# A graph-attention layer: spreading the maxima in four wide products, and issuing the gathers in one piece at the head of a step

## The chip, the cores and the metric

The kernel runs on one core of one Trainium2 chip. The metric is the device time of one execution in microseconds (us); lower is better. The time before is the median of three runs, 1335.21 us, with the runs between 1331.93 and 1343.83 us. Five engines work beside each other, each through its own instruction queue in program order: TensorE (PE), VectorE (DVE), ScalarE (ACT), GpSimd (POOL) and SyncE (SP). Transfers are issued from SP, ACT and POOL.

## The reference

Inputs are 3125 nodes with 128 features, 100000 edges (`src`, `dst`, sorted by `dst`) and for each edge one of five types. For each type `r` the reference computes an 8-head attention over the edges of that type, and adds the five results:

```
q, k, v = x[dst] @ W_Q[r], x[src] @ W_K[r], x[src] @ W_V[r]        # per edge, 8 heads of 16
logits  = (q * k).sum(-1) / 4 + attn_bias[r]
max_v   = segment_max(logits of type r, dst)
exp_l   = exp(logits - max_v[dst])                                  # 0 for other types
attn    = exp_l / (segment_sum(exp_l, dst)[dst] + 1e-12)
out    += segment_sum(attn * v, dst)
```

After that come an output projection with bias, a residual, a layer norm with gain and shift, a second residual with `x` and a second layer norm.

## The kernel before, in words

**Prologue.** All keys and values for each (node, type) pair are computed first and stored in DRAM as `kv_d`: row `5 * node + type`, 256 numbers (K, then V). The queries go to `q_d` in three bf16 parts that add up to the exact number. The list of rows to gather for each edge lies in SBUF as `idx[p, t, g]`.

**Groups and windows.** The edges, sorted by destination, are cut into 196 groups of 512 (`NGR`, `GE`): four columns `t` of 128 edges (`T = 4`). The destinations of one group lie within 25 nodes, so a group touches at most 125 rows (25 nodes by 5 types) of `q_d` and of the table of maxima `m_d`.

**The loop.** Loop step `k` works on several groups at different stages; which groups is fixed by `group_at`, `v_at`, `full_step`, `ready` and `done_at`, and the order of calls in the body of `for k in range(...)` is the program order on every engine. For a group `g` the stages are:

- `gather` (POOL, L681): four indirect DMAs bring the K and V rows of 4 x 128 edges into the ring of buffers `kvs_[g % KVB]`. The first `KVA` groups are gathered ahead of the loop; in the loop, step `k` issues those of group `k + AHEAD`, `AHEAD` being 2. The first two of a group are issued after `weigh`, the other two after `logits`, and these two take their row numbers from a small copy `rows` that VectorE makes (L692).
- `spot` (DVE, L746) makes `hot`, a 0/1 matrix that says which of the 125 rows each edge belongs to; `spread_q` (PE, L755) multiplies `hot` by the three parts of the queries, so that each edge has its query, `qe`.
- `logits` (DVE, L768 and L769), in step `g`: product of keys and queries, then a sum over each head; `store_logits` (SP) writes them to `lg_d`.

When all logits of a block of 128 nodes are there, in step `full_step[b]`, the block's maxima follow. `maxima_load` (POOL, L781) fetches the logits by node into `ell` with one indirect DMA, in step `full_step[b] + 1`. `maxima` (DVE and ACT, L796 to L840) takes the masked maxima in three pieces at the end of steps `full_step[b] + 2` to `+ 4`; its first instructions, `by_head` on ACT and `mine` on DVE, wait for `ell`. The result, in three bf16 parts for each head, is stored to `m_d` (`store_m`) and read back by group (`fetch_m`, tile `mw`).

Then the same edges come by a second time, as group `v`. From group 22 on, that is 19 steps after their logits:

- `spread_m` (PE, L872), one step ahead: `hot` times the three parts of the maxima, accumulated in PSUM, gives each edge its maximum, tile `me`. The operand repeats the 8 heads `times` times (8 times in the loop, so 64 columns; 12 times after the last group), and only the first repetition is read.
- `less_max` (DVE, L881) and `exps` (ACT, L885): the exponentials, written in place over `me` in PSUM.
- `weigh` (DVE, L890), in step `at_k[v]`: values times exponentials, to `wv`. It is the last reader of the group's gathered buffer. `weights` (ACT, L898) copies the exponentials beside them.
- `places` (ACT), `sums` (PE, L924 and on), `norm` (DVE, L945 to L948), `carry` and `by_node`: sums by row, division, sum over the types.

**What ties the gathers to the rest.** With `KVB = 21` buffers, the gathers of group `k + 2` go into the buffer of group `k - 19`, which `weigh` releases in step `k` itself. The copies `rows` and the gathers that read them are also tied: the second half of the gathers of group `k + 2` can't start before DVE has passed `logits` of step `k`. On POOL's queue the order is: the first two gathers of group `k + 2`, the other two, then, once every eight steps, `maxima_load`.

Of the kernel before, what the change touches and what calls it, by code (L numbers as in the profile page):

```python
# [17 lines left out]
P = 128  # L18
# [4 lines left out]
HEADS = 8  # L23
# [17 lines left out]
T = GE // P  # L41
NGR = -(-E // GE)
# [4 lines left out]
WR = WN * R  # L47
# [6 lines left out]
AHEAD = 2  # L54
# [5 lines left out]
SB = P * E // N // SR  # L60
SPAD = 5
QB = 3
KVB = 21
HELD = 21
KVA = 6


@with_exitstack
# [61 lines left out]
NM = len(MB)  # L130


def windowed_path(
# [4 lines left out]
    nc = tc.nc  # L138
# [4 lines left out]
    kv_d = dram.tile([((NT - 1) * P + 64) * R, KVW], F32, name="kv_d")  # L143
# [208 lines left out]
    live = {}  # L352
# [290 lines left out]
    rows, counted = {}, 0  # L643
# [29 lines left out]
    ps = ctx.enter_context(tc.tile_pool(name="ps", bufs=2, space=PSUM))  # L673
    buffers(i for i in range(KVB) if i not in at_once)
    hold = ctx.enter_context(tc.tile_pool(name="hold", bufs=HELD))
    flow = ctx.enter_context(tc.tile_pool(name="flow", bufs=2))
    late_flow = ctx.enter_context(tc.tile_pool(name="late_flow", bufs=2))
    def gather(g, t0, rows):
        kv = kvs_[g % KVB]
        for t in range(T // 2):  # L680
            nc.gpsimd.indirect_dma_start(  # L681
                out=kv[:, t0 + t, :], out_offset=None, in_=kv_d[:, :],
                in_offset=bass.IndirectOffsetOnAxis(ap=rows(t), axis=0),
            )

    def first_gathers(g):
        gather(g, 0, lambda t: idx[:, t, g : g + 1])

    def more_gathers(g):

        rows = flow.tile([P, T // 2], I32, name="rows", bufs=3)
        nc.vector.tensor_copy(rows, idx[:, T // 2 :, g])  # L692
        gather(g, T // 2, lambda t: rows[:, t : t + 1])


    def fetch_x(name, b):
# [68 lines left out]
    def logits(g):  # L765
        kv, lg = kvs_[g % KVB], live["lg", g]
        prod = flow.tile([P, T, H], F32, name="prod", bufs=1)
        nc.vector.tensor_tensor(prod, kv[:, :, :H], live.pop(("qe", g)), op=ALU.mult)  # L768
        nc.vector.tensor_reduce(  # L769
            lg[:, :, :HEADS], prod.rearrange("p t (k d) -> p t k d", d=HD), AX.X, ALU.add  # L770
        )
# [7 lines left out]
    def maxima_load(b):  # L779
        ell = late_flow.tile([P, D, LW], F32, name="ell", bufs=1)  # L780
        nc.gpsimd.indirect_dma_start(  # L781
            out=ell.rearrange("p s c -> p (s c)"), out_offset=None,
            in_=lg_d[: (full_at(MEND[b], D) + 1) * GE, :],
            in_offset=bass.IndirectOffsetOnAxis(ap=start_i[:, b : b + 1], axis=0),
        )
        live["ell", b] = ell
# [78 lines left out]

    def spread_m(g, times):

        me = ps.tile([P, T, times, 2, HEADS // 2], F32, name="me", tag="me")
        hot, mw = live.pop(("hot", g)), live.pop(("mw", g))
        for t in range(T):  # L870
            for s in range(3):
                nc.tensor.matmul(  # L872
                    me[:, t], hot[:, t, :],
                    mw[:WR, None, :, s, :].to_broadcast([WR, times, 2, HEADS // 2]),
                    start=(s == 0), stop=(s == 2),
                )
        live["mde", g] = me[:, :, 0].rearrange("p t h k -> p t (h k)")

    def less_max(g):
        mde = live["mde", g]  # L880
        nc.vector.tensor_tensor(mde, live.pop(("lg", g))[:, :, :HEADS], mde, op=ALU.subtract)  # L881

# [4 lines left out]
    def weigh(g):  # L887
        wv, kv = late_flow.tile([P, T, PW], F32, name="wv"), kvs_[g % KVB]
        live["wv", g] = wv
# [66 lines left out]
    def by_node(g):  # L956
        f = window(g, first, ACTE)
        nc.scalar.copy(oT[:, bass.ds(f, WN)], live.pop(("op", g)))
# [68 lines left out]
    step_of, n = {}, 0  # L1027
# [3 lines left out]
    group_at = {k: g for g, k in step_of.items()}  # L1031
    final = step_of[NGR - 1]
# [5 lines left out]
    full_step = [step_of[full_at(n, D)] for n in MEND]  # L1038
# [3 lines left out]
    at_k, k = {}, 0  # L1042
    for v in range(NGR):
        k = max(k + 1, ready[block_of(v, MEND)])
        at_k[v] = k
    v_at = {k: v for v, k in at_k.items()}
# [19 lines left out]

    gathered = 0
    for gathered in range(KVA):
        first_gathers(gathered)
        gather(gathered, T // 2, lambda t: idx[:, T // 2 + t, gathered : gathered + 1])  # L1070
    assert all(q_from[b] >= 2 for b in range(QB, NT))
    for k in range(-2, root_at[NT] + 2):
        v, g = v_at.get(k), group_at.get(k)
        q_step = {k - f: b for b, f in enumerate(q_from) if b >= QB and -2 <= k - f <= 5}

        if k >= 0 and k + 3 in group_at:
            fetch_keys(group_at[k + 3])
            fetch_q(group_at[k + 3])
        if -2 in q_step:
            fetch_x("xq", q_step[-2])  # L1080
        for b in range(NT):
            if done_at[b] - 1 == k:
                fetch_x("xr", b)
            if norm_at[b + 1] + 1 == k:
                store_z(b)
        for b in range(NM):
            if ready[b] - 3 == k:
                store_m(b)
        if 5 in q_step:
            store_q(q_step[5])  # L1090
        for u in range(NGR):
            if max(at_k[u] - 3, ready[block_of(u, MEND)] - 2) == k:
                fetch_m(u)

        for b in range(NT):
            if done_at[b] + 1 == k:
                residual(b)
        if v_at.get(k - 4) is not None:
            by_node(v_at[k - 4])
        if v_at.get(k - 2) is not None:  # L1100
            carry(v_at[k - 2])
        if 1 in q_step:
            turned(q_step[1])
        if 3 in q_step or 4 in q_step:
            second_part()
        if 2 in q_step or 3 in q_step:
            first_part()

        if v_at.get(k + 1) is not None:
            spread_m(v_at[k + 1], 8 if k + 1 in group_at else 12)  # L1110
        if v_at.get(k - 1) is not None or v_at.get(k - 3) is not None:
            sums(v_at.get(k - 1), v_at.get(k - 3))
        if k + 1 in group_at:
            spread_q(group_at[k + 1])

        if v is not None:
            weigh(v)
        ahead_of = []
        while gathered < NGR - 1 and step_of[gathered + 1] <= k + AHEAD:
            gathered += 1  # L1120
            ahead_of.append(gathered)
            first_gathers(gathered)
        if v_at.get(k + 1) is not None:
            less_max(v_at[k + 1])
            exps(v_at[k + 1])
        if v is not None:
            weights(v)
        if k + 1 in group_at:
            types(group_at[k + 1])
        if v_at.get(k - 2) is not None:  # L1130
            norm(v_at[k - 2])
        if g is not None:
            logits(g)
            store_logits(g)
        for u in ahead_of:
            more_gathers(u)
        for b in range(NM):
            if full_step[b] + 1 == k:
                maxima_load(b)
        if k + 2 in group_at:  # L1140
            spot(group_at[k + 2])
        if v_at.get(k + 1) is not None:
            places(v_at[k + 1], 2 if k >= final - 1 else 0)
        if 3 in q_step or 4 in q_step:
            third_part()
        if 2 in q_step or 3 in q_step:
# [528 lines left out]
```

## Time and profile before

| | us |
|---|---|
| median of three runs | 1335.21 |
| lowest and highest run | 1331.93, 1343.83 |
| the profiled execution: its own time | 1331.93 |
| the profiled execution: its span, first to last instruction | 1330.1 |
| busy: PE, DVE, ACT, POOL | 873.1, 958.6, 633.8, 802.4 |
| mean granted TensorE clock | 0.762 |

The span is one execution on the core. "Busy" is the time with an instruction of that engine running. An idle time is put down to the thing that ended it, written `A <- B`. A line such as L681 is a line of the kernel above. The chain that ended last is followed back from the last instruction, at each step to what released it.

The execution has four stretches: the prologue to 84 us, a start-up in which gathers are issued back to back to about 240 us, the steady loop until the last gather is issued at 1243.84 us, and an end without gathers.

### The profile page before, as it was taken

Reading aid. Unit: us, or ns where it says so; the run is one execution under the profiler, and the core shown is the slowest. Engines: PE = TensorE matmul, PEld = TensorE weight load, DVE = VectorE, ACT = ScalarE, POOL = GpSimd, SP = SyncE. Lnnn points to the kernel's source line nnn. Section 1 sums busy time; section 2 is a strip of 40 time slices with the busy share of each in tenths; the row PEclk is TensorE's granted clock in tenths of the full one; section 3 lists DMA queues with packets and bytes.
Section 4 is the critical chain, followed back from the end, with each engine's and each line's share of the span. In section 5 each row is a group of like instructions: output and inputs, shape, how many; then the busy total and the mean of one; then the engine's idle time right before and its main releaser. Section 6 shows DMA issues by size and latency. Waiting matters only on the chain.

```text
span 1330.1 us, 26045 instructions
## 1 busy us (share of the span) xinstructions
PE 873.1 (66%) x7526; PEld 685.6 (52%) x7526; DVE 958.6 (72%) x2749; ACT 633.8 (48%) x2248; POOL 802.4 (60%) x901
## 2 busy tenths in 40 slices
PE   7974356576667676665757656667766677676595
PEld 3543244455455555544645545555545565565474
DVE  4554557768777876876976876877787687687786
ACT  2650034355446445445545545545644544544354
POOL 2637776666667667567656656766766766666300
PEclk9985577787688778778777868877767866776787
DMA  6986676566566556456556556656645655655300
GB/s 171 352 301 169 160 180 147 151 167 157 137 158 167 133 152 170 124 153 175 128 146 168 149 132 162 153 145 163 165 135 150 177 131 146 168 138 136 82 10 17
DMA packets 180892, 203.66 MB, mean 153 GB/s; under 512 B 83207, under 2 KB 146083, under 8 KB 180620
## 3 DMA queue, kind: packets, MB, share of 16 engines
q0 software_dynamic: 40896, 113.39, 29.6%
q1 hardware_dynamic: 135414, 83.80, 26.2%
q10 hardware_dynamic: 4430, 4.71, 1.4%
q8 instruction: 63, 1.03, 0.3%
q14 instruction: 89, 0.73, 0.2%
HBM read 166.50 MB, written 35.28 MB: 152 GB/s over the span
## 4 chain that ended last, share of the span: by engine, by line
DVE 34%; PE 21%; DMA 20%; issue 12%; POOL 7%; ACT 4%; SPq 2%; DVEq 0%; ACTq 0%; POOLq 0%
DMA ell<-lg_d,start_i 8%; POOL kv L681 7%; PE pp L924 6%; DVE wl L819 5%; DVE prod L768 4%; DMA mw<-m_d 4%; DVE wv L890 4%; PE pr L395 3%; DVE mx L825 3%; PE me L872 3%; DVE lg L769 3%; DVE hot L746 2%; PE qe L755 2%; ACT by_head L796 2%; DMA kv<-kv_d,rows 2%
## 5 line engine op out<-in xcount | busy, mean ns | idle before, releaser
L681 POOL DMA_INDIRECT kv<-kv_d,idx x404 | 383.8, 950 | 261.8 <-DVE den L945 142.8
L681 POOL DMA_INDIRECT kv<-kv_d,rows x380 | 363.8, 957 | 131.9 <-issue 76.6
L924 PE MATMUL pp<-wv,at 128*125 128x136 f32 x1568 | 357.6, 362 | 1.0 <-DVE o L948 1.0
L924 PEld LDWEIGHTS pp<-wv,at 128*125 128x125 f32 x1568 | 267.8, 236 | 66.1 <-issue 64.2
L910 ACT ACTIVATE at<-row_at,nkey 128x125 f32<-128x125 f32 x744 | 237.5, 397 | 0.0
L755 PE MATMUL qe<-qw,hot 125*128 125x128 bf16 x2352 | 206.9, 251 | 40.9 <-DVE hot L746 36.5
L872 PE MATMUL me<-mw,hot 125*128 125x64 bf16 (+1 forms) x2352 | 125.7, 210 | 143.6 <-DMA mw<-m_d 69.5
L755 PEld LDWEIGHTS <-hot 125*128 125x128 bf16 x2352 | 194.0, 123 | 47.4 <-DVE hot L746 44.1
L885 ACT ACTIVATE me<-me 128x32 f32<-128x32 f32 x196 | 35.7, 182 | 365.8 <-DVE me L881 364.7
L872 PEld LDWEIGHTS <-hot 125*128 125x128 bf16 x2352 | 112.9, 109 | 176.4 <-DVE wv L890 77.1
L926 PE MATMUL pp<-pt,carried 125*5 125x136 f32 x390 | 96.0, 337 | 135.4 <-ACT pt L939 135.0
L768 DVE TENSOR_TENSOR prod<-kv,qe 128x512 f32<-128x512 f32 x196 | 133.1, 679 | 61.5 <-DMA kv<-kv_d,rows 49.5
L769 DVE TENSOR_REDUCE lg<-prod 128x32 f32<-128x512 f32 x196 | 134.4, 686 | 6.8
L890 DVE TENSOR_TENSOR wv<-kv,me 128x512 f32<-128x512 f32 x196 | 132.2, 675 | 4.9 <-PE pp L924 4.3
L913 ACT ACTIVATE at<-at 128x500 f32<-128x500 f32 (+1 forms) x196 | 117.3, 598 | 6.2
L716 PE MATMUL prq<-wq,xTq 128*128 128x384 f32 (+1 forms) x88 | 51.4, 680 | 98.5 <-DVE rem L726 98.5
L926 PEld LDWEIGHTS pp<-pt,carried 125*5 125x5 f32 x390 | 18.2, 86 | 174.2 <-ACT pt L939 153.4
L796 ACT COPY by_head<-ell 128x512 f32<-128x512 f32 x24 | 25.7, 1071 | 139.9 <-DMA ell<-lg_d,start_i 139.9
L804 DVE SCALAR_TENSOR_TENSOR mine<-slot,deg,ell 128x64 f32<-128x64 f32 x25 | 8.4, 336 | 115.5 <-DMA ell<-lg_d,start_i 115.5
L881 DVE TENSOR_TENSOR me<-lg,me 128x32 f32<-128x32 f32 x196 | 37.3, 191 | 74.4 <-PE me L872 70.7
L819 DVE TENSOR_TENSOR wl<-by_head,shut 128x1024 f32<-128x1024 f32 (+2 forms) x73 | 76.9, 1053 | 11.5 <-ACT by_head L796 9.3
L746 DVE TENSOR_SCALAR hot<-kt,row_of 125x512 bf16<-125x512 bf16 x196 | 82.7, 422 | 1.5 <-DMA kv<-kv_d,idx 1.0
(186 smaller groups left out, 1210.7 us busy)
## 6 DMA issues: line engine op xcount, KB each, us to landing
kt<-key_d SPq DMA_DIRECT2D x196, 128.0 KB
qw<-q_d SPq DMA_DIRECT2D x196, 96.0 KB
kv_d<-kvs SPq DMA_DIRECT2D x24, 640.0 KB
q_d<-q SPq DMA_DIRECT2D x22, 480.0 KB
kv<-kv_d,idx POOLq DMA_INDIRECT x404
kv<-kv_d,rows POOLq DMA_INDIRECT x380
lg_d<-lg SPq DMA_DIRECT2D x196, 18.0 KB
mw<-m_d SPq DMA_DIRECT2D x196, 6.0 KB
```

Of the source, the lines that this page charges most:

```text
L681: nc.gpsimd.indirect_dma_start(out=kv[:, t0 + t, :], out_offset=None, in_=kv_d[:, :], in_offset=bass.IndirectOffsetOnAxis(ap=rows(t), axis=0),
L746: nc.vector.tensor_scalar(hot, live.pop(("kt", g))[:WR], row_of[:WR], None, op0=ALU.is_equal)
L755: nc.tensor.matmul(qe[:, t, :], hot[:, t, :], qw[:WR, s, :], start=(s == 0), stop=(s == 2))
L768: nc.vector.tensor_tensor(prod, kv[:, :, :H], live.pop(("qe", g)), op=ALU.mult)
L769: nc.vector.tensor_reduce(lg[:, :, :HEADS], prod.rearrange("p t (k d) -> p t k d", d=HD), AX.X, ALU.add)
L819: nc.vector.tensor_tensor(wl, by_head[:, None].to_broadcast([P, n, nh, D]), shut[:, :n, None, :].to_broadcast([P, n, nh, D]), op=ALU.add,)
L872: nc.tensor.matmul(me[:, t], hot[:, t, :], mw[:WR, None, :, s, :].to_broadcast([WR, times, 2, HEADS // 2]), start=(s == 0), stop=(s == 2),)
L890: nc.vector.tensor_tensor(wv[:, :, :H].rearrange("p t (k d) -> p t k d", d=HD), kv[:, :, H:].rearrange("p t (k d) -> p t k d", d=HD), live ...
L910: nc.scalar.activation(at[:, t, :], row_at[:, :WR], AF.Abs, bias=nkey[:, t, g : g + 1], scale=1.0)
L913: nc.scalar.activation(at[:, on_dve:], at[:, on_dve:], AF.Relu, bias=1.0, scale=-1.0)
L924: nc.tensor.matmul(pp, at[:, t, :], wv[:, t, :], start=(t == 0), stop=(t == T - 1))
L926: nc.tensor.matmul(pp[:R], carried[:WR, g, :], live.pop(("pt", g - 1)), start=False, stop=False,)
```

## The change

Three things are changed, and two sizes.

1. `spread_m` inside the loop: one product per column `t` with all three parts side by side (5 repetitions of 24 columns, 120 columns), instead of three accumulating products of 64 columns. So 4 products instead of 12 per step. `less_max` first adds up the three parts with a VectorE reduction from PSUM into an SBUF tile `mde`, and the subtraction, the exponential, `weigh` and `weights` work on `mde` in SBUF from there. After the last group (12 repetitions) all stays as it was.
2. The four gathers of a group are issued in one piece, with their row numbers read from `idx` directly; the copy `rows` is gone. They stand at the head of a step, before the step's `weigh`, with `maxima_load` right behind them. In the last 16 steps before the last group they are issued for group `k + 1` instead of `k + 2`.
3. `KVB` is 22 instead of 21, and `KVA`, the groups gathered ahead of the loop, 9 instead of 6.

```diff
-KVB = 21
+KVB = 22
-KVA = 6
+KVA = 9
...
-    def gather(g, t0, rows):
+    def gather(g):
         kv = kvs_[g % KVB]
-        for t in range(T // 2):
+        for t in range(T):
             nc.gpsimd.indirect_dma_start(
-                out=kv[:, t0 + t, :], out_offset=None, in_=kv_d[:, :],
-                in_offset=bass.IndirectOffsetOnAxis(ap=rows(t), axis=0),
-            )
-
-    def first_gathers(g):
-        gather(g, 0, lambda t: idx[:, t, g : g + 1])
-
-    def more_gathers(g):
-
-        rows = flow.tile([P, T // 2], I32, name="rows", bufs=3)
-        nc.vector.tensor_copy(rows, idx[:, T // 2 :, g])
-        gather(g, T // 2, lambda t: rows[:, t : t + 1])
+                out=kv[:, t, :], out_offset=None, in_=kv_d[:, :],
+                in_offset=bass.IndirectOffsetOnAxis(ap=idx[:, t, g : g + 1], axis=0),
+            )
...
     def spread_m(g, times):
+        hot, mw = live.pop(("hot", g)), live.pop(("mw", g))
+        if times < 8:
+            me = ps.tile([P, T, times, 2, 3, HEADS // 2], F32, name="me", tag="me")
+            for t in range(T):
+                nc.tensor.matmul(
+                    me[:, t], hot[:, t, :],
+                    mw[:WR, None].to_broadcast([WR, times, 2, 3, HEADS // 2]),
+                    start=True, stop=True,
+                )
+            live["parts", g] = me[:, :, 0].rearrange("p t h s k -> p t h k s")
+            return
...
     def less_max(g):
+        if ("parts", g) in live:
+            mde = flow.tile([P, T, 2, HEADS // 2], F32, name="mde")
+            nc.vector.tensor_reduce(mde, live.pop(("parts", g)), AX.X, ALU.add)
+            live["mde", g] = mde.rearrange("p t h k -> p t (h k)")
...
                 fetch_m(u)
+        while gathered < NGR - 1 and step_of[gathered + 1] <= k + (AHEAD if k < final - 16 else 1):
+            gathered += 1
+            gather(gathered)
+        for b in range(NM):
+            if full_step[b] + 1 == k:
+                maxima_load(b)
...
-            spread_m(v_at[k + 1], 8 if k + 1 in group_at else 12)
+            spread_m(v_at[k + 1], 5 if k + 1 in group_at else 12)
...
             weigh(v)
-        ahead_of = []
-        while gathered < NGR - 1 and step_of[gathered + 1] <= k + AHEAD:
-            gathered += 1
-            ahead_of.append(gathered)
-            first_gathers(gathered)
...
             store_logits(g)
-        for u in ahead_of:
-            more_gathers(u)
-        for b in range(NM):
-            if full_step[b] + 1 == k:
-                maxima_load(b)
```

More of the change, by code (lines that the diff above doesn't have):

```diff
@@ L866, in spread_m @@
     def spread_m(g, times):
+        hot, mw = live.pop(("hot", g)), live.pop(("mw", g))
[9 more added lines that the diff above has]
+            return
         me = ps.tile([P, T, times, 2, HEADS // 2], F32, name="me", tag="me")
-        hot, mw = live.pop(("hot", g)), live.pop(("mw", g))
         for t in range(T):
@@ L1068, in windowed_path @@
     for gathered in range(KVA):
-        first_gathers(gathered)
-        gather(gathered, T // 2, lambda t: idx[:, T // 2 + t, gathered : gathered + 1])
+        gather(gathered)
     assert all(q_from[b] >= 2 for b in range(QB, NT))
@@ L1093, in windowed_path @@
                 fetch_m(u)
+        while gathered < NGR - 1 and step_of[gathered + 1] <= k + (AHEAD if k < final - 16 else 1):
+            gathered += 1
+            gather(gathered)
+        for b in range(NM):
+            if full_step[b] + 1 == k:
+                maxima_load(b)
         for b in range(NT):
@@ L1117, in windowed_path @@
             weigh(v)
-        ahead_of = []
-        while gathered < NGR - 1 and step_of[gathered + 1] <= k + AHEAD:
-            gathered += 1
-            ahead_of.append(gathered)
-            first_gathers(gathered)
         if v_at.get(k + 1) is not None:
```

## The prediction, made before the changed kernel was run

> **What bounds the kernel now.** I read the page's chain first, since it says which waits are on the path, then the waits of VectorE and GpSimd in the steady loop (240 to 1150 us), then one place of the timeline where they meet. The chain by line, from the page:
>
> ```profile
> DMA ell<-lg_d,start_i 8%; POOL kv L681 7%; PE pp L924 6%; DVE wl L819 5%; DVE prod L768 4%; DMA mw<-m_d 4%; DVE wv L890 4%; PE pr L395 3%; DVE mx L825 3%; PE me L872 3%; DVE lg L769 3%; DVE hot L746 2%; PE qe L755 2%; ACT by_head L796 2%; DMA kv<-kv_d,rows 2%
> ```
>
> No engine is full (DVE has 72%, POOL 60%), and the largest single item is a transfer, the load of `ell`. The waits of 240 to 1150 us (total us, times, longest) say who pays:
>
> ```profile
> DVE mine L804 <- DMA ell<-lg_d,start_i: 93.5, 19, 6.1
> DVE me L881 <- PE me L872: 62.0, 44, 3.9
> DVE prod L768 <- DMA kv<-kv_d,rows: 18.0, 20, 2.4
> ...
> POOL kv L681 <- DVE den L945: 129.2, 56, 5.3
> POOL kv L681 <- issue: 117.3, 384, 0.6
> ```
>
> Once a block (19 times) VectorE stands 4.9 us for `ell`. And POOL, which should bring it, stands 129.2 us for VectorE. The "issue" line is POOL's own 0.30 us between two gathers: a gather is 0.95 + 0.30 = 1.25 us, a group 5.0 us, and a block of eight groups and one `ell` 33 x 1.25 = 41.3 us, busy or not. The period of a block is 242.3 / 5 = 48.4 us (five blocks, 582.5 to 824.8 us, in which DVE is busy 183.14 us, 36.6 a block). So neither engine fills the period: they take turns. In the timeline (start, duration):
>
> ```profile
> 575.89 0.50 DVE L746 TENSOR_SCALAR hot<-kt,row_of 125x512 bf16<-125x512 bf16 x1
> 581.46 0.33 DVE L804 SCALAR_TENSOR_TENSOR mine<-slot,deg,ell 128x64 f32<-128x64 f32 x1 [5.07 <-DMA ell<-lg_d,start_i]
> ...
> 586.43 0.68 DVE L890 TENSOR_TENSOR wv<-kv,me 128x512 f32<-128x512 f32 x1
> ...
> 576.58 0.95 POOL L781 DMA_INDIRECT ell<-lg_d,start_i  x1 [0.31 <-issue]
> ...
> 581.58 1.04 POOL L681 DMA_INDIRECT kv<-kv_d,rows  x1 [0.30 <-issue]
> 587.38 0.94 POOL L681 DMA_INDIRECT kv<-kv_d,idx  x1 [4.77 <-DVE den L945]
> ```
>
> POOL issues `ell` late, because gathers stand before it. VectorE waits 5.07 us; then it does the maxima and ends `weigh` at 587.11, and only 0.27 us later POOL goes on: it has waited 4.77 us for the buffer that `weigh` frees (the profile names `den`, but that had begun just before; the buffer is `weigh`'s). In light steps (3 us from `weigh` to `weigh`) POOL's 5.0 us a group falls behind; in heavy ones (6 us) it may not run ahead.
>
> **The change, part by part**, against the profiled execution's 1331.9 us (span 1330.1, 1.8 outside).
>
> *One step of lead.* With 22 buffers and the gathers ahead of `weigh`, group `k + 2` needs the buffer of group `k - 20`, freed by `weigh` of step `k - 1`, not `k`; and no half waits for `rows`. I walk one block, in us from `weigh` of the step after the maxima's first piece. The `weigh` starts of the old steps are 5.9, 6.3, 3.6, 5.5, 5.0, 3.0, 3.2 and 15.8 us apart. With 0.2 added to each for the reduction and 0.35 off the fourth (both below), they fall at 0, 6.1, 12.6, 16.4, 21.7, 26.9, 30.1 and 33.5. The gathers of the group that completes the next block may start 0.95 us (0.68 + 0.27) after the third of these, at 13.5; from there POOL runs four groups back to back to 33.5, then `ell`, which lands 4.9 us after its start (576.58 to 581.46): 38.4. VectorE asks for it about 5.5 us after the last `weigh`, at 39.0 (576.39 - 570.37 = 6.0 in the old block, 0.34 less for gathered rows, 0.35 less for PE, 0.2 more). So `ell` comes just in time, if the stored logits are there: their reduction ends near 30.1, the store takes 2.7 to 3.9 us by the chain, and SP can lag by some 2 us (a store issued at 572.34 for a reduction that ended at 570.13). I leave 1 us of the 4.9 standing (bounds 0 and 2.5).
>
> The terms for 240 to 1150 us:
> - Wait for `ell`: 93.5 goes, 19 x 1 stays: -74.5 (bounds -93.5 and -46).
> - Wait for gathered rows: -18.0, since the rows now land 7 us or more ahead.
> - The reduction, 128x96 to 128x32, isn't in the trace. From its nearest rows, 512 elements in 686 ns and 1024 in 1220:
>
> ```profile
> L769 DVE TENSOR_REDUCE lg<-prod 128x32 f32<-128x512 f32 x196 | 134.4, 686 | 6.8
> L825 DVE TENSOR_REDUCE mx<-wl 128x16 f32<-128x1024 f32 x48 | 58.6, 1220 | 1.7
> L692 DVE COPY rows<-idx 128x2 int32<-128x2 int32 x190 | 35.9, 189 | 0.0
> L872 PE MATMUL me<-mw,hot 125*128 125x64 bf16 x2124 | 111.5, 209 | 135.7 <-DMA mw<-m_d 69.2 <-ACT wv L898 50.7 <-ACT pt L939 6.1
> L755 PE MATMUL qe<-qw,hot 125*128 125x128 bf16 x2352 | 206.9, 251 | 40.9 <-DVE hot L746 36.5 <-DMA kv<-kv_d,idx 1.9 <-DMA qw<-q_d 1.4
> ```
>
>  a line gives 152 + 1.04 x 96 = 252 ns, and 30 more since the subtraction depends on it: 150 x 0.28 = +42. Bounds: 0 (where VectorE waited for PE anyway) and 150 x 0.69 = +103; the line lies nearest.
> - The copy `rows`: 189 ns, but `hot` starts 0.07 us behind it (575.82, 575.89): -11; bounds -11 and -29. The net of the two is +0.2 a step.
> - PE: 12 products of 64 columns took 0.57 to 0.85 us; 12 of 128 columns 0.83 to 1.46, so four of 120 take 0.26 to 0.46. That is 0.35 less, and it counts in the 44 waits of VectorE for `me`: -15. PE is busy 66% there; elsewhere its gain is hidden. The PSUM tile is also freed a step earlier, by the reduction instead of `weights`; PE then waits at `sums`, which needs the same `weigh`: nothing.
> - `less_max`, `exps`, `weigh`, `weights` on SBUF instead of PSUM: nothing, by these two rows, the upper with two SBUF inputs and the lower with one in PSUM:
>
> ```profile
> L735 DVE TENSOR_TENSOR q<-rem,q 128x384 bf16<-128x384 f32 x22 | 11.9, 543 | 0.0
> L726 DVE TENSOR_TENSOR rem<-prq,q 128x384 f32<-128x384 f32 x22 | 11.9, 542 | 0.0
> ```
>
>  The bound on the other side is the last rival below. The ACT pieces run beside VectorE; with no row for them in SBUF I leave some 0.1 us either way, under ACT's idle time (25 us busy of 48 in a block).
>
> Sum: -74.5 - 18 + 42 - 11 - 15 = -76.5. Cross-check by the walk: period 33.5 + 9.9 + 1 = 44.4 (the last step: 15.8 less 4.9, 0.95 and 0.35, plus 0.2), 4.0 us less, in 910 / 48.4 = 18.8 blocks 75 us.
>
> Other stretches. 1150 to 1270: `ell` costs 14.4 in three waits, the last of which hangs on the last block's maxima; two shrink to 1 each, -8; rows -5.1; 15 steps of +0.2, +3; together -10. The shorter reach of the last 16 steps only changes POOL's order, in `ell`'s favour. Before 240: POOL is back to back (105 us for 80 instructions from 135 to 240, 100 of them its own), so VectorE's additions hide under it and nothing is won. `KVA` 9: groups 6 to 8 had already followed without a wait at 118.71, so nothing. After 1270: unchanged code.
>
> Total -86.5: 1245 us for this execution. The median of the runs shown is 3.3 above it, so 1249.
>
> **A rule against it.** With both inputs in SBUF, rows L735 and L726 show no difference beside gathers that run 0.95 of every 1.25 us. The Trainium skill, page SBUF — State Buffer, section Who interferes with whom, says that a Vector instruction with two SBUF inputs contends with a GpSimd instruction that reads SBUF, and that one blocks the other entirely; `weigh` and `less_max` become such instructions. By the row the cost is nothing; by the rule it is the last rival's, and I go by the row.
>
> **A second rule, on PE's clock.** The granted clock was 0.55 where PE was busy 22.48 of 51 us (84 to 135), and 0.76 at 606.36 of 910. The changed block would have (32.0 - 2.8) / 44.4 = 66%, as now, so I leave the clock. The page TensorE: Matmul & The Clock Gate, section Part 1: The HAM clock gate, says that the clock follows PE's recent activity and halves after an idle window; by it the fewer columns alone would cost clock, the shorter period gives it back.
>
> **The rivals.**
> 1. *The lead is too short.* It grows by one step only, and `ell` still stands behind all four gathers. For it: the margin in the walk is 0.6 us. Against: POOL starts a whole step earlier. Then 2.5 us of each `ell` wait stay (+32 over 21 blocks) and the row waits return (+18): 1249 + 50 = 1299. Chance 0.15.
> 2. *POOL alone sets the pace.* Its 809 issues of 1.25 us from 88.3 end at 1100 instead of 1246, which allows -146. VectorE with its 36.6 + 1.6 us a block would have to lose most `me` waits as well; half-way there, -120: 1215. Chance 0.10.
> 3. *The change doesn't free POOL*: the buffers still hold it in step, the waits stay as they are, and +42 - 11 - 15 = +16 is left: 1351, or about no change if part of the waits goes. Chance 0.07.
> 4. *Slower: the gathers hold up VectorE.* If `weigh` and `less_max` wait out a running gather, each loses on average 0.95 / 2 x 0.76 = 0.36 us, 0.72 a step, over 165 steps +119: 1249 + 119 = 1368. From 86.5 / 165 = 0.52 us a step it decides against the change. Chance 0.10.
>
> **The numbers.** The forecast (1225 to 1272, by the bounds of `ell` and the reduction) has 0.58. Adding the most of rivals 1 and 2, the range is 1208 to 1310. Faster by over 1% holds the forecast and rivals 1 and 2, 0.83; within 1% a part of rival 3, 0.05; slower the rest, 0.12. About 1% is what a measurement of this kernel tells from no change.
>
> **What would show it.** The period of a block near 44 us; VectorE's wait for `ell` near 1 us a block, its waits for gathered rows gone; POOL waiting for VectorE under 2 us a block; the reduction near 250 ns; four products of 120 columns under 0.5 us; `weigh` still 675 ns. `ell` waits of 3 us and more would make rival 1 true, a `weigh` above 0.9 us rival 4. What would break the forecast is above all that a later transfer (`mw`, `lg_d`) takes `ell`'s place in the chain.

## The result, and the profile after

| | before | after |
|---|---|---|
| median (lowest to highest), us | 1333.78 (1331.93 to 1343.83) | 1264.56 (1260.54 to 1266.57) |
| profiled execution, us | 1331.93 | 1260.54 |
| VectorE, 151 steps: whole, busy, idle | 914.07, 694.47, 219.6 | 856.95, 713.61, 143.3 |
| POOL's waits for VectorE in the same steps, all lines added up | 184.5 | 59.9 |

The ratio is 0.946, with a 95% interval of 0.941 to 0.952. The 151 steps are those between the 11th and the 162nd `weigh`, the start of which is found in the timeline of each kernel: from 249.61 to 1163.68 us before, from 246.37 to 1103.32 us after. They are the stretch that the prediction called 240 to 1150, cut at the same instruction in both, and they serve for every comparison below.

The chain that ended last, by line, after the change:

```profile
POOL kv L681 14%; DMA kv<-kv_d,idx 12%; DMA ell<-lg_d,start_i 6%; DVE prod L759 4%; DVE wl L810 4%; PE pp L929 3%; PE pr L395 3%; DVE wv L895 3%; DVE mx L816 2%; DVE lg L760 2%; DMA mw<-m_d 2%; ACT by_head L787 2%; DVE hot L737 2%; DVE mde L883 1%; DMA kt<-key_d 1%
```

POOL's gathers have come to the front, and `ell` has not left the chain: 6% where it had 8%. The waits of VectorE, POOL and SP in the 151 steps (total us, times, longest):

```profile
DVE mine L795 <- DMA ell<-lg_d,start_i: 41.6, 17, 3.5
DVE mde L883 <- PE me L863: 28.9, 23, 3.5
DVE mde L883 <- ACT q L712: 17.7, 15, 1.2
...
DVE prod L759 <- DMA kv<-kv_d,idx: 1.0, 4, 0.3
...
POOL kv L681 <- issue: 147.7, 483, 0.6
POOL kv L681 <- DVE mde L883: 40.1, 49, 1.6
POOL ell L772 <- DMA kt<-key_d: 9.7, 6, 2.4
POOL ell L772 <- ACT pt L944: 8.6, 5, 2.0
POOL ell L772 <- DMA lg_d<-lg: 8.2, 3, 3.2
...
SPq L730 <- DMA qw<-q_d: 55.2, 19, 3.6
```

Before, cut in the same way, `ell` stood at 93.0 us in 19 waits, `me` at 62.0 in 44, the gathered rows at 15.6. At the gathers POOL now runs nearly unchecked: most of its idle time is its own 0.30 us between them. At the 19 loads of `ell` it stands 32.1 us in all, where it stood 5.8 before (0.30 us each, its own). The last line, on SP's queue, becomes the point of an experiment below. The groups that the change made or touched, over the whole execution (busy us, mean ns, then the idle time ahead and its releasers):

```profile
L681 POOL DMA_INDIRECT kv<-kv_d,idx x784 | 762.0, 972 | 281.8 <-issue 192.5 <-DVE mde L883 43.7 <-DMA kv_d<-kvs 13.6
L895 DVE TENSOR_TENSOR wv<-kv,mde 128x512 f32<-128x512 f32 x177 | 120.1, 678 | 0.2 <-PE pp L929 0.2
L863 PE MATMUL me<-mw,hot 125*128 125x120 bf16 x708 | 83.6, 254 | 68.5 <-DMA mw<-m_d 68.2
L883 DVE TENSOR_REDUCE mde<-me 128x32 f32<-128x96 f32 x177 | 44.5, 251 | 57.1 <-PE me L863 39.3 <-ACT q L712 17.7
```

`weigh` with both inputs in SBUF takes 678 ns beside gathers that run all the time, and the reduction 251 ns. One block in the timeline (start, duration, and in brackets the idle time before and what ended it), SP first, then POOL and VectorE:

```profile
720.41 0.34 SPq L373 DMA_DIRECT2D qw<-q_d  x1
723.78 0.34 SPq L730 DMA_DIRECT2D q_d<-q  x1
724.64 0.34 SPq L853 DMA_DIRECT2D mw<-m_d  x1
725.09 0.44 SPq L765 DMA_DIRECT2D lg_d<-lg  x1
...
731.13 0.94 POOL L772 DMA_INDIRECT ell<-lg_d,start_i  x1 [3.16 <-DMA lg_d<-lg]
...
722.97 0.69 DVE L760 TENSOR_REDUCE lg<-prod 128x32 f32<-128x512 f32 x1
...
730.69 0.26 DVE L883 TENSOR_REDUCE mde<-me 128x32 f32<-128x96 f32 x1 [2.94 <-PE me L863]
734.93 0.33 DVE L795 SCALAR_TENSOR_TENSOR mine<-slot,deg,ell 128x64 f32<-128x64 f32 x1 [1.50 <-DMA ell<-lg_d,start_i]
```

POOL gets to `ell` early enough, but the stored logits aren't there: it stands 3.16 us. By the program order, the last store that this `ell` needs is that of 725.09, and the reduction that makes these logits had ended at 723.66. Ahead of it stood the store of the next queries (480 KB, L730), which itself had stood from 720.75 to 723.78 behind the load of queries. The load of maxima (`mw`) stood behind the same store, and VectorE waited 2.94 us for the products that need it.

### The profile page after: what moved, and what is told of

The parts are those of the page before. It is cut to its first block, busy times and chain, and to the rows that moved or that the text cites. A ratio compares the mean times of both kernels' runs of the same rounds, so it can differ in the third digit from the quotient of the medians.

```text
span 1258.8 us, 22885 instructions
## 1 busy us (share of the span) xinstructions
PE 860.0 (68%) x6110; PEld 662.1 (53%) x6110; DVE 980.9 (78%) x2736; ACT 645.0 (51%) x2248; POOL 817.3 (65%) x901
## 4 chain that ended last, share of the span: by engine, by line
DVE 28%; DMA 24%; POOL 14%; PE 13%; issue 12%; ACT 6%; SPq 1%; DVEq 0%; ACTq 0%; POOLq 0%
POOL kv L681 14%; DMA kv<-kv_d,idx 12%; DMA ell<-lg_d,start_i 6%; DVE prod L759 4%; DVE wl L810 4%; PE pp L929 3%; PE pr L395 3%; DVE wv L895 3%; DVE mx L816 2%; DVE lg L760 2%; DMA mw<-m_d 2%; ACT by_head L787 2%; DVE hot L737 2%; DVE mde L883 1%; DMA kt<-key_d 1%
## 5 line engine op out<-in xcount | busy, mean ns | idle before, releaser
L681 POOL DMA_INDIRECT kv<-kv_d,idx x784 | 762.0, 972 | 281.8 <-issue 192.5
L746 PEld LDWEIGHTS <-hot 125*128 125x128 bf16 x2352 | 199.4, 125 | 48.4 <-DVE hot L737 45.9
L890 ACT ACTIVATE mde<-mde 128x32 f32<-128x32 f32 x177 | 40.6, 229 | 352.8 <-DVE mde L886 345.0
L863 PE MATMUL me<-mw,hot 125*128 125x120 bf16 x708 | 83.6, 254 | 68.5 <-DMA mw<-m_d 68.2
L895 DVE TENSOR_TENSOR wv<-kv,mde 128x512 f32<-128x512 f32 x177 | 120.1, 678 | 0.2 <-PE pp L929 0.2
L863 PEld LDWEIGHTS <-hot 125*128 125x128 bf16 x708 | 59.6, 118 | 101.2 <-DMA mw<-m_d 75.6
L883 DVE TENSOR_REDUCE mde<-me 128x32 f32<-128x96 f32 x177 | 44.5, 251 | 57.1 <-PE me L863 39.3
L938 PEld LDWEIGHTS pp<-rsum,o 125*128 125x128 f32 x392 | 79.8, 247 | 4.6 <-issue 4.1
L816 DVE TENSOR_REDUCE mx<-wl 128x16 f32<-128x1024 f32 (+2 forms) x73 | 76.5, 1048 | 2.5
L737 DVE TENSOR_SCALAR hot<-kt,row_of 125x512 bf16<-125x512 bf16 x196 | 74.6, 381 | 1.8 <-DMA kt<-key_d 1.0
L938 PE MATMUL pp<-rsum,o 125*128 125x25 f32 x392 | 71.3, 265 | 4.2 <-DVE o L953 4.2
```

The source lines that it names most:

```text
L681: nc.gpsimd.indirect_dma_start(out=kv[:, t, :], out_offset=None, in_=kv_d[:, :], in_offset=bass.IndirectOffsetOnAxis(ap=idx[:, t, g : g + ...
L746: nc.tensor.matmul(qe[:, t, :], hot[:, t, :], qw[:WR, s, :], start=(s == 0), stop=(s == 2))
L863: nc.tensor.matmul(me[:, t], hot[:, t, :], mw[:WR, None].to_broadcast([WR, times, 2, 3, HEADS // 2]), start=True, stop=True,)
L895: nc.vector.tensor_tensor(wv[:, :, :H].rearrange("p t (k d) -> p t k d", d=HD), kv[:, :, H:].rearrange("p t (k d) -> p t k d", d=HD), live ...
L938: nc.tensor.matmul(op, live.pop(("o5", done)), rsum[:WR], start=True, stop=True)
```

## The experiments

The kernels ran on several chips, each beside the kernel before on the same chip. On two of them the kernel before took 1338.77 and 1338.45 us, much as where the change was first measured; on two others, which were used first, 1551.03 and 1516.22 us. The former settle the account, so they are told first.

### The new spread alone

To the kernel before, `spread_m` and `less_max` of the changed kernel; the gathers untouched.

```diff
+        if times < 8:
+            me = ps.tile([P, T, times, 2, 3, HEADS // 2], F32, name="me", tag="me")
...
+        if ("parts", g) in live:
+            mde = flow.tile([P, T, 2, HEADS // 2], F32, name="mde")
+            nc.vector.tensor_reduce(mde, live.pop(("parts", g)), AX.X, ALU.add)
...
-            spread_m(v_at[k + 1], 8 if k + 1 in group_at else 12)
+            spread_m(v_at[k + 1], 5 if k + 1 in group_at else 12)
```

> The kernel before with the new spread of the maxima alone. Where the kernel before takes 1334 us: by the terms of the prediction +42 for the reduction, -15 for PE, +10 about for the ends, some of it hidden where VectorE waits for ell anyway: 1340 to 1375, ratio 1.005 to 1.03. Rival (the products of 12 x 64 were on the path far more often than 44 times): below 1325. Where the kernel before takes 1516 us and more: 0.975 to 1.003, as on the two chips before.

Measured: 1357.03 us against 1338.77, ratio 1.014 (1.013 to 1.016). So this half of the change costs 18 us by itself, inside the expected range and against the rival. The waits of VectorE in the 151 steps of this kernel:

```profile
DVE mine L804 <- DMA ell<-lg_d,start_i: 95.0, 19, 6.0
DVE mde L892 <- PE me L872: 27.4, 19, 2.8
DVE mde L892 <- ACT q L721: 18.1, 15, 1.5
DVE prod L768 <- DMA kv<-kv_d,rows: 17.8, 17, 2.9
```

The wait for `ell` is what it was (93.0 before). Those of the first instruction that reads `me` go from 62.0 to 27.4 + 18.1 = 45.5, by their main lines. VectorE's busy time grows from 694.47 to 720.86, by 26.4. That is less than the reduction takes, since the instructions that make `hot` became shorter at the same time (their rows in the 151 steps, before and with the new spread):

```profile
L746 DVE TENSOR_SCALAR hot<-kt,row_of 125x512 bf16<-125x512 bf16 x152 | 65.4, 430 | 0.0
...
L892 DVE TENSOR_REDUCE mde<-me 128x32 f32<-128x96 f32 x151 | 38.0, 252 | 48.1 <-PE me L872 27.4 <-ACT q L721 18.1 <-ACT pt L953 2.4
L746 DVE TENSOR_SCALAR hot<-kt,row_of 125x512 bf16<-125x512 bf16 x152 | 54.5, 359 | 0.0
```

The reduction adds 38.0 us and `hot` gives 10.9 back, which was no part of the plan; the last section has more on it. The 151 steps take 935.07 us, 21.0 more than before.

### The lead taken back

To the changed kernel: 21 buffers, and the gathers with the load of `ell` moved back behind `weigh`.

```diff
-KVB = 22
+KVB = 21
...
-        while gathered < NGR - 1 and step_of[gathered + 1] <= k + (AHEAD if k < final - 16 else 1):
-            gathered += 1
-            gather(gathered)
-        for b in range(NM):
-            if full_step[b] + 1 == k:
-                maxima_load(b)
...
             weigh(v)
+        while gathered < NGR - 1 and step_of[gathered + 1] <= k + (AHEAD if k < final - 16 else 1):
+            gathered += 1
+            gather(gathered)
+        for b in range(NM):
+            if full_step[b] + 1 == k:
+                maxima_load(b)
```

> The changed kernel with the lead taken back: 21 buffers, the four gathers and the load of ell behind weigh instead of ahead of it; the gathers still without halves, copies and lockstep, and the new spread. Where the kernel before takes 1334 us: theory (the step of lead is what won, not the absence of the lockstep) 18 blocks x 2.4 us of ell waits and 18 us of row waits return, 1265 + 60 = 1325, within 1310 to 1340; rival (the absence of the copies and the lockstep won) 1265 to 1285. Where the kernel before takes 1516 us and more: if the longer lead is what made the changed kernel slow there (1547), this one is near the kernel with the new spread alone, 1515 to 1525; if the lockstep is what protects the kernel before, it stays at 1540 to 1560.

Measured: 1331.89 us against 1338.77, ratio 0.996 (0.994 to 0.997): the theory, not the rival. The waits of VectorE and POOL in the 151 steps:

```profile
DVE mine L795 <- DMA ell<-lg_d,start_i: 94.1, 19, 6.5
...
DVE prod L759 <- DMA kv<-kv_d,idx: 16.7, 18, 2.2
...
POOL kv L681 <- DVE mde L883: 140.1, 71, 5.9
```

All three are back near the values of the kernel before (93.0, 15.6 and 129.2). Against the changed kernel the 151 steps are 62.8 us longer (919.74 and 856.95) at the same busy time of VectorE (713.47 and 713.61), so the whole gain of the lead is idle time, and `ell` (52.5) and the rows (15.7) account for it. Against the new spread alone, this kernel is 25 us faster: 15.3 in these steps, the rest at the two ends. It differs from that kernel by the copies and halves, by the nine groups gathered ahead and by the shorter reach at the end, and no run takes these apart.

### The query store behind the logits store

To the changed kernel: in the same step, but behind the load of maxima and the store of logits on SP's queue.

```diff
-        if 5 in q_step:
-            store_q(q_step[5])
...
             logits(g)
             store_logits(g)
+        if 5 in q_step:
+            store_q(q_step[5])
```

> The changed kernel with the 480 KB store of the next queries put behind the step's store of logits on SP's queue, instead of ahead of the stored maxima's load and that store. Theory (the query store holds up the stored logits that ell gathers): where the kernel before takes 1334 us, VectorE's wait for ell falls from 2.5 us a block to 1 or less, 18 blocks, so about -25: 1235 to 1245, ratio 0.925 to 0.933. Rival (a load behind it on SP's queue, of keys, queries or maxima, comes late in its place): the ell wait falls, mw or qw rises, 1255 to 1270. Where the kernel before takes 1516 us and more, the changed kernel took 1547: theory 1515 to 1535, rival 1540 to 1560.

Measured: 1237.37 us against 1338.77, ratio 0.924 (0.922 to 0.926), where the changed kernel stands at 0.946. The time is the theory's. The waits in the 151 steps:

```profile
DVE mine L795 <- DMA ell<-lg_d,start_i: 27.0, 18, 3.0
...
DVE den L950 <- ACT pt L944: 17.2, 19, 1.0
...
DVE mde L883 <- PE me L863: 9.0, 10, 2.9
...
POOL ell L772 <- issue: 4.9, 16, 0.3
...
SPq L730 <- DMA qw<-q_d: 5.5, 7, 1.3
```

SP's stand ahead of the query store has gone from 55.2 us (2.9 a block) to 5.5. The way is not quite the theory's, though: `ell` falls to 1.4 us a block and not to 1 (-14.6 in all), and the larger part comes from the maxima, which had been queued behind the same store: the wait for `me` falls by 19.9. Some 12 of that turn into a wait for ACT at `den`. POOL stands 8.2 us at the 19 loads of `ell` where it stood 32.1, and in 17 of these blocks the store that `ell` needs is issued less than 0.1 us after its reduction, where it came 1.4 us after it on average in the changed kernel. So the store no longer explains the 27.0 us that VectorE still waits for `ell`: POOL comes to it at its own pace, and an order of its work that would bring `ell` earlier was not tried on these chips. The 151 steps take 832.88 us, 24 less than in the changed kernel.

### The old spread in that version

To the version just told: `spread_m` and `less_max` of the kernel before, so 12 products of 64 columns and no reduction. Of the edit, the line of the call:

```diff
-            spread_m(v_at[k + 1], 5 if k + 1 in group_at else 12)
+            spread_m(v_at[k + 1], 8 if k + 1 in group_at else 12)
```

> The last version (query store behind the logits store) with the old spread of the maxima, 12 products of 64 columns into PSUM, in place of 4 of 120 and the reduction; the gathers as changed. It tells what the spread is worth once ell no longer waits. Where the kernel before takes 1339 us (with the new spread this version took 1237): theory by the terms of the prediction, VectorE at 85% now has the 0.25 us reduction on its path in some 150 steps: -0.28 x 150 = -42 at most, of which POOL's pace leaves a part, and +15 for PE: 1205 to 1232. Rival (the 12 products come late for VectorE oftener once it no longer waits for ell, and PE's clock sinks): 1245 to 1275. Where the kernel before takes 1516 us and more, the old spread was 3% slower than the new one with the same gathers: 1560 to 1600.

Measured: 1210.21 us against 1338.45, ratio 0.904 (0.900 to 0.908). This beats both kernels of the case. It lies in the theory's range. The waits of VectorE, and a row of the table of windows (stretch, its length, then busy us and instructions of PE, PE's weight loads, DVE, ACT and POOL, the granted clock, the share of DMA and GB/s):

```profile
DVE me L872 <- PE me L863: 40.7, 31, 2.9
DVE mine L795 <- DMA ell<-lg_d,start_i: 27.6, 17, 2.6
...
245.63:1059.55 813.92, 583.39 (x5634) 473.13 (x5633) 672.17 (x1841) 474.46 (x1681) 598.28 (x630) 0.80 0.67 171
```

The same row with the new spread:

```profile
247.37:1080.25 832.88, 585.62 (x4426) 463.40 (x4424) 710.71 (x1991) 483.28 (x1681) 613.00 (x630) 0.77 0.66 166
```

Without the reduction VectorE is busy 38.5 us less; it waits 19.6 us more in all, 14.0 of them at `me` (40.7, against 9.0 for PE and 17.7 for `q` on ACT at the reduction); 19.0 us are won here, and by the ratios 27 in the whole (0.020 x 1338). TensorE has 1200 products more and the same busy time, beside a granted clock of 0.80 instead of 0.77.

### Two chips on which the sign turns

Four kernels ran on the chip where the kernel before took 1551.03 us, and three of them again, together with the changed kernel, where it took 1516.22. The first theories were written for a chip on which it takes 1335 us, so that only the ratios bear on them.

*The gathers alone*: the changed kernel with the old spread. Of the edit, the line of the call:

```diff
-            spread_m(v_at[k + 1], 5 if k + 1 in group_at else 12)
+            spread_m(v_at[k + 1], 8 if k + 1 in group_at else 12)
```

> The changed kernel with the old spreading of the maxima (12 products of 64 columns, accumulated; exponentials in PSUM, no reduction on VectorE); gathers, buffers and the place of the load of ell as changed. Theory (the gain is POOL's lead; the new spreading costs VectorE its reduction): faster than the changed kernel by the reduction less PE's gain, 42 - 15 = 27 us, so about 1235 us, ratio to before about 0.925. Rival (the smaller work on PE brings a good part of the gain): slower than the changed kernel, 1285 us or more.

*The new spread alone*, the same kernel as above.

> The kernel before with the new spreading alone (4 products of 120 columns, the reduction on VectorE, exponentials in SBUF); gathers in two halves, 21 buffers, as before. Theory: +5 to +27 us, 1338 to 1360, since VectorE gets 0.28 us more a step and only the part beside its waits is free. Rival (the smaller work on PE, or the PSUM tile freed earlier, brings a good part of the gain): 1315 us or less.

*The query work two steps earlier*: aimed at the same store as the experiment that settled it.

```diff
-        f = step_of[min(g for g in range(NGR) if min(block_of(g) + 1, NT - 1) >= b)] - 10
+        f = step_of[min(g for g in range(NGR) if min(block_of(g) + 1, NT - 1) >= b)] - 12
```

> The changed kernel with the queries of a block made and stored two steps earlier (12 steps ahead of their first use instead of 10), so that the 480 KB store of q_d no longer stands just ahead of the fetch of mw and of the store of the block's last logits on SP's queue. Theory (what is left of the wait for ell, 2.5 us a block, and of the wait for PE's me is set by that store): VectorE's wait for ell falls from 45 to under 20 us and its wait for me from 29 to under 15 in the steady stretch, the time by 25 to 40 us, to 1225 to 1240. Rival (it is set by the gathers that stand ahead of ell on POOL): no change within 5 us.

*Shorter reach in all steps*, so that `ell` has fewer gathers ahead of it.

```diff
-        while gathered < NGR - 1 and step_of[gathered + 1] <= k + (AHEAD if k < final - 16 else 1):
+        while gathered < NGR - 1 and step_of[gathered + 1] <= k + 1:
```

> The changed kernel with the gathers issued for group k + 1 instead of k + 2 in all steps: POOL's order changes so that one group fewer (5 us of POOL) stands ahead of each ell; the buffers bind as before. Theory (ell waits for the logits' store): no gain, 0 to +15 us, as POOL then stands at ell for the store with fewer gathers done. Rival (ell waits for the gathers ahead of it): the wait for ell goes, -30 to -40 us, to 1220 to 1235.

The changed kernel itself, and three of these kernels, on the other chip:

> The changed kernel once more, beside the kernel before on one chip, as the base for the three runs with it, since the chip of the first four runs gave the kernel before 1551 us instead of 1334. On a chip where the kernel before takes about 1334: 1262, ratio 0.946. On a chip like that one: by the theory that POOL's back-to-back gathers hold up everything else there, 1640 to 1660, ratio about 1.06; by the rival that only the two edits of those runs hurt, a ratio below 1.

> The changed kernel with the old spreading of the maxima. On a chip where the kernel before takes about 1334: theory (the gain is POOL's lead; the new spreading costs VectorE its reduction) about 1235 us, ratio about 0.925, below the changed kernel; rival (the smaller work on PE brings a good part of the gain) 1285 us or more. On a chip like the first: above the kernel before again, by 5%.

> The kernel before with the new spreading alone. On a chip where the kernel before takes about 1334: theory +5 to +27 us, 1338 to 1360; rival (the smaller work on PE or the earlier free PSUM tile brings a good part of the gain) 1315 us or less. On a chip like the first: 2 to 3% below the kernel before again.

> The changed kernel with the queries of a block made and stored two steps earlier. On a chip where the kernel before takes about 1334: theory (the rest of the wait for ell and for me is set by the 480 KB store ahead of them on SP's queue) VectorE's wait for ell from 45 to under 20 us and for me from 29 to under 15 in the steady stretch, 1225 to 1240 us; rival (it is set by the gathers ahead of ell on POOL) within 5 us of the changed kernel.

Ratios to the kernel before on the same chip, with intervals:

| kernel | before at 1551.03 | before at 1516.22 | before at 1334 to 1339 |
|---|---|---|---|
| the changed kernel | not run | 1.017 (1.009 to 1.024) | 0.946 (0.941 to 0.952) |
| gathers alone | 1.051 (1.045 to 1.057) | 1.053 (1.047 to 1.058) | not run |
| new spread alone | 0.975 (0.969 to 0.982) | 1.003 (1.000 to 1.005) | 1.014 (1.013 to 1.016) |
| query work earlier | 1.059 (1.048 to 1.070) | 1.067 (1.061 to 1.072) | not run |
| shorter reach | 1.060 (1.051 to 1.069) | not run | not run |

On these chips the gathers' half costs instead of bringing time, and the new spread costs nothing or brings some. Of what was expected of the second chip, the gathers alone came true (5% above); the changed kernel, at 1.017, lies between its theory (1.06) and its rival (below 1); and the new spread alone missed (2 to 3% below was expected, 1.003 measured). The instructions themselves are as long as elsewhere (the gathers 947 to 1008 ns, `weigh` 678 to 683). What differs is the idle time, which is put down to "remote" or "issue", that is, to no release that the profile has. VectorE with the gathers alone, where the kernel before took 1551, between 246 and 1400 us:

```profile
DVE me L872 <- remote: 203.4, 29, 21.9
DVE me L872 <- PE qe L746: 76.9, 14, 8.2
```

And the start of its loop, with the last of POOL's gathers there:

```profile
121.64 0.69 DVE L759 TENSOR_TENSOR prod<-kv,qe 128x512 f32<-128x512 f32 x1 [18.25 <-issue]
...
154.48 0.69 DVE L759 TENSOR_TENSOR prod<-kv,qe 128x512 f32<-128x512 f32 x1 [31.18 <-remote]
...
149.48 0.95 POOL L681 DMA_INDIRECT kv<-kv_d,idx  x1 [0.30 <-issue]
```

POOL issues gathers without a pause until 150.4 us, and VectorE does one `prod` at 121.64 and the next only at 154.48. In the changed kernel where it was first measured, beside the same unbroken gathers, six `prod` start from 121.64 to 147.07 us, each after a wait of 0.9 to 4.3 us for its rows. The spread is not what makes the difference, for the changed kernel itself has the same hole on the chip where the kernel before took 1516:

```profile
116.96 0.69 DVE L759 TENSOR_TENSOR prod<-kv,qe 128x512 f32<-128x512 f32 x1 [14.69 <-issue]
149.11 0.69 DVE L759 TENSOR_TENSOR prod<-kv,qe 128x512 f32<-128x512 f32 x1 [30.48 <-remote]
```

A reading that fits in part: on these chips other engines learn late of transfers that have landed while POOL issues without pause, and a kernel that lets POOL run ahead suffers more. It isn't shown: the traces there have few of the landings, no run took the gathers' pace as its one variable, and in the lines just shown `prod` comes back at 149.11, while POOL's last gather (148.60, 0.95 long) still runs. What sets these chips apart stays open. The two experiments on `ell` of this group (query work earlier, shorter reach) thus say nothing about the chip of the result.

## Why the prediction was right, and which terms were off

The predicted 1249 us stands against 1264.56, in the range and on the side given 0.83. Term by term, over the 151 steps, from the waits and busy times above:

| term | predicted, us | measured, us |
|---|---|---|
| wait for `ell` | -74.5 | 93.0 to 41.6: -51.4 |
| wait for gathered rows | -18.0 | 15.6 to 1.0: -14.6 |
| waits at `me` (PE, 12 products to 4) | -15 | 62.0 to 28.9 + 17.7: -15.4 |
| VectorE's work: reduction, and copies gone | +42 - 11 | 694.47 to 713.61: +19.1 |
| other waits | 0 | the rest: +5.2 |
| sum | -76.5 | -57.1 |

The stretch before these steps gave -3.2 where nothing was expected, the end -10.9 where -10 was: -71.3 of the profiled span, against -86.5.

**The term that was mis-sized is the wait for `ell`.** The step reads: "So `ell` comes just in time, if the stored logits are there", with SP late by some 2 us, and 1 us a block left standing between bounds of 0 and 2.5. It measured 2.2. The walk of POOL held: in 18 of 19 blocks POOL reached `ell` before it could issue it, and it stood there 1.4 us a block beyond its own 0.30. The condition was what failed, and the step's own terms would have said so: a reduction that ends near 30.1, a store issued 2 us later and at least 2.7 us to land make 34.8, while POOL is there at 33.5. The prediction had seen SP's lag, in the store issued at 572.34. The store that `ell` needed there was the one before it, issued 2.3 us after its reduction, and right behind the query store:

```profile
565.97 0.69 DVE L769 TENSOR_REDUCE lg<-prod 128x32 f32<-128x512 f32 x1
...
567.65 0.34 SPq L739 DMA_DIRECT2D q_d<-q  x1
568.50 0.34 SPq L862 DMA_DIRECT2D mw<-m_d  x1
568.95 0.39 SPq L774 DMA_DIRECT2D lg_d<-lg  x1
```

So the lag was no accident of one step but the query store, which stood 2.9 us a block on SP's queue for the load ahead of it, 57.0 us in the kernel before and 55.2 after. Moving it gave some 30 us by the ratios (0.0224 x 1334), of which the smaller part came at `ell`: 14.6 of the 41.6 us went, and 27.0 stayed with POOL hardly held up. What sets these is not shown; POOL's pace is what is left. The sentence on what would break the forecast ("a later transfer (`mw`, `lg_d`) takes `ell`'s place in the chain") was near: in the chain neither took its place (`ell` has 6%, `mw` 2%), but both were late behind that store.

**VectorE's work.** The reduction's 251 ns are the line's 252, and it adds 38 us of busy time. The copies' -11 measured -7.4 (720.86 to 713.47 with the lead taken back). What the prediction had no term for is `hot`: its rows sum to 65.4 us in the 151 steps before and 57.7 after. So the smaller +19.1 is in part luck. In time, the spread alone cost 18.3 us, and 27 by the ratios in the last experiment; there the two terms of the prediction come out nearly as they were put, 38.5 us of work for 42 and 14.0 us of waits for 15.

**The waits at `me`.** The number is met, -15.4 for -15, but not by the way that was given, 0.35 us less in each of 44 waits. In the 151 steps the products of a step took 0.63 us on average before (0.52 to 0.85) and 0.47 after (0.37 to 0.61, not the 0.26 to 0.46 of the estimate), which makes 0.16 x 44 = 7 us. PE's own waits for `weights` ahead of these products, 39.4 us before, are gone after; the prediction put the earlier free PSUM tile at nothing. How the rest of the 15 divides is not shown.

**The signs.** The period of a block is 45.1 us (five blocks, from the `ell` at 550.04 to that at 775.53), for 44.4; the last step of the prediction's cross-check adds up to 9.8 and not 9.9, which changes nothing. The waits for rows are gone, and `weigh` and the reduction are as stated. POOL waits 3.2 us a block for VectorE and not under 2, and the four products take over 0.5 us in 66 of 152 steps.

**The rivals.** The first (lead too short) was half true: the `ell` waits of 2.2 us are near its 2.5, but the row waits did not return, and part of the cause was SP's queue; how much of the rest is the four gathers ahead of `ell` no run on these chips shows. The second (POOL alone sets the pace) is near only in the last version: POOL's last gather starts at 1178 us in the changed kernel, 1156 with the store moved, 1133 with the old spread, and the prediction's floor was 1100. The third is refuted, as POOL's waits for VectorE fell from 184.5 to 59.9 us. The fourth, the slower one, is refuted where the gathers were expected to hold up VectorE: `weigh` takes 678 ns against 675 before, and the subtraction of `less_max` 192 against 191. The Trainium skill's rule, page SBUF — State Buffer, section Who interferes with whom, speaks of such contention; no run here shows it for these two instructions, whether the gathers are sparse or unbroken. Another instruction of VectorE, `hot`, is longer beside the gathers in both kernels, as the last section tells.

**PE's clock.** For the whole change the prediction left the clock as it was, and so it is: 0.762 and 0.764 in the two profiled executions. The halves taken apart move it: beside 0.756 for the kernel before (median of the runs on that chip), the new spread alone has 0.738, and 0.790 goes with the old spread in the shorter period, where the kernel before had 0.754. PE is busy 67% of the 151 steps before, 65% with the new spread alone and 72% in the last version. The Trainium skill, page TensorE: Matmul & The Clock Gate, section Part 1: The HAM clock gate, has the clock follow PE's recent activity; the direction agrees, and the runs show no more than the mean, which moves by 0.02 to 0.04.

## What to carry to other kernels

When a wait on the critical path is to go, follow the awaited transfer back through every queue that it passes, not only the engine that issues it: here the gather was made early enough, and a store that waited on SP's queue, ahead of what the gather and PE needed, kept some 30 us of the gain. Test the parts of a joint change one by one, also when the whole is faster: here, by the ratios, one part won 90 us (1.014 to 0.946) and the other gave 18 to 27 back. An engine that will become the bound (VectorE rose from 76% of the 151 steps to 83%, and to 85% with the store moved) should not be given work to relieve one that is not.

## What the runs showed of the hardware that was not expected

The kernel before took 1333.78, 1338.77 and 1338.45 us in three comparisons and 1551.03 and 1516.22 us in two others, on different chips, each within 1%. The changed kernel, worth -5% on the chip of the result, was worth +2% where the kernel before took 1516, and its half with the longer lead +5% on both chips of that kind. A verdict on a kernel that hangs on the timing of many small gathers is thus one about where and when it ran, too. Each chip of the experiments was used on one occasion, so the chip and the occasion can't be told apart. The times of different chips were compared here by their ratios to the kernel before on the same chip; the waits and busy times in the 151 steps are taken side by side only where the kernel before took 1334 to 1339.

One instruction of VectorE is longer or shorter by the moment at which it starts. `hot` takes 0.34 us at its shortest, and up to 0.57 in the kernel before and 0.58 after. In the 151 steps of the kernel before, all 72 that took more than 0.40 us began 0.4 to 0.7 us after a gather had started on POOL, and ended near 1.06 us after that start. With the new spread alone 11 were as long, and 28 in the changed kernel, all of them in the same place beside a gather. Of those that began in that stretch of a gather, 8 stayed under 0.40 us in the kernel before, 26 after. The products of 128x512, `weigh` and `prod`, show nothing of the kind (0.63 to 0.70 us in both kernels). So a change that only moves instructions against each other went with some 10 us of busy time here; why a gather does this to `hot` and not to the products, no run shows.
